# The transposed h of the last two packs, made from a transposed x by elementwise passes

## The chip, the cores and the metric

The kernel runs on one core of one Trainium2 chip. The metric is the device time of one execution in microseconds (us); the median of three runs of the kernel before is 2174.33 us (2174.08 to 2176.43). All data are 32-bit floats.

## What is computed

Two layers over a graph of 3327 nodes with 512 features. `_layernorm` has no weights of its own.

```
h = maximum(_layernorm(x), 0)
q, k, v = h @ Wq.T + bq, h @ Wk.T + bk, h @ Wv.T + bv
a = q @ k.T / sqrt(512) + adj + adj
x = x + softmax(a) @ v

h = maximum(_layernorm(x), 0)
A2 = adj + eye
dscale = diagonal(A2) ** -0.5
x = x + relu((dscale[:, None] * A2 * dscale[None, :]) @ (A2 @ h @ W.T))
```

The change concerns the first two lines: h, in the transposed form in which the query projection and the scores use it.

## The kernel before, in words

The nodes are padded to 26 tiles of 128 rows. A half holds 13 tiles. Matrix products are done in Strassen's manner (Winograd's form): of two halves of one side and two halves of the other, seven products of sums and differences in place of eight. The key projection is folded into the query side, M = Wq.T Wk, so that the scores are h (h M).T.

**First stage, to about 112 us.** The tiles of a half are put into four packs (`PACKS`, L213) of 4, 3, 3 and 3; a pack stands for its tiles in both halves, so 8, 6, 6 and 6 tiles. They are taken in the order `TURN` = (1, 2, 0, 3). "Third" and "fourth" below are pack 0 (8 tiles, products of 512 columns) and pack 3 (6 tiles, products of 384 columns).

`h_transposed(k)` (L304) makes a pack's transposed h in `hp[k]`, a tile of seven parts: a11, a12 (0, 1) from the first half of the nodes, a22 (2) from the second, and the sums S1 to S4 (3, 4, 5, 6), into which a21 goes. For each tile it loads x (L275, on SP's DMA queue, into a ring of 11 buffers), takes mean and variance on VectorE (`norm`, L191 to L200) with the power -1/2 on GpSimd (L200), applies scale, bias and Relu on ScalarE (L311) into `ht` (a ring of four buffers), stores `ht` to DRAM for the later stages (`rowd`, L312), turns it by four transposes on TensorE (`tp`, L315) into one bank of PSUM, and gets it out by copies on ScalarE (L318, L320) and sums on VectorE (L321, L322, and L324, L325 once for a pack).

`project_q(k)` (L327) multiplies a pack's seven parts by the seven parts of M, in two chains (o = 0, 1), one for each half of a quarter's outputs. The order within a chain is that of `Chain` (L231):

```
product(Y, "m1", True);  first(0, Y, -1)
product(Z, "p5", True);  first(3, Z, -1)
product(X, "p2", True);  more(0, X)
product(Y, "p6", False); first(1, Y, -1)
Chain.finish()
product(Z, "p3", False); more(1, Z)
product(Y, "p7", False); more(3, Y)
```

`Chain.finish()` does the p4, `first(2)` and `last()` of the chain before. X, Y and Z are banks of PSUM. A product with `False` adds to what its bank holds, so it must come after the read of the bank ahead of it. `first` is a read on ScalarE (L341), `more` a read on VectorE (L344); both write into `qs[0..3]` (L331), each of which has a single buffer, used again by the next pack. `last`, in the second chain alone, stores the four to DRAM (`qd`, L351) from SP's queue. As a chain's p4 and `last` come inside the next chain, those of a pack's second chain come inside the next pack.

The loop at L388 to L392 calls `h_transposed` for the next pack and then `project_q` for the one before it. In this stage the order of the instructions on each engine is chosen by a planner, which takes ready instructions by the order in which they were written; nothing is fixed by hand. So transposes of the next pack lie between the products of this one.

**Later stages.** The scores (from L397, products at L467) load the queries back from `qd` (`queries`, L404, into buffers `half` 0, 14, 1 and 2), and there and in the three large products after (L826, L818) every engine's order is fixed by hand with `in_order` (L91): each instruction is made to follow the one before it on its engine.

Of the kernel before, what the change touches and what calls it, by code (L numbers as in the profile page):

```python
# [35 lines left out]
HALF = 13  # L36
# [7 lines left out]
ROW = tuple(STRIPS[s] + y * HT[s] + k for y in range(2) for s in range(2) for k in range(HT[s]))  # L44
# [3 lines left out]
def graph_layers_kernel(  # L48
    ctx: ExitStack,
    tc: tile.TileContext,  # L50
    x: bass.AP,
    adjT: bass.AP,
    wq: bass.AP,
    wk: bass.AP,
# [22 lines left out]
    nc = tc.nc  # L77
# [28 lines left out]
    def half(k, shape, name):  # L106
        return arena.tile(shape, F32, name=name, tag=f"half{k}")
# [58 lines left out]
    totd = dram.tile([1, NP], F32, name="totd")  # L166
    x1d = [dram.tile([P, D], F32, name=f"x1d{i}") for i in range(NT)]
    rowd = [[dram.tile([P, D], F32, name=f"row{g}_{i}") for i in range(NT)] for g in range(3)]
    t2d = [[dram.tile([P, 4, P], F32, name=f"t2{g}_{t}") for t in range(PAIRS + 1)] for g in range(3)]

    def four_sums(o, g):
# [16 lines left out]
        lo, hi = max(r0, c0), min(r0 + P, c0 + a.shape[-1])  # L188
        return (slice(lo - c0, hi - c0), ident[:, lo - r0 : hi - r0]) if lo < hi else None

    def norm(src):  # L191

        st = small.tile([P, 6], F32, name="st")
        nc.vector.bn_stats(st, src)
        mv = small.tile([P, 2], F32, name="mv")
        nc.vector.bn_aggr(mv, st)
        ve = small.tile([P, 1], F32, name="ve")
        nc.vector.tensor_scalar(ve, mv[:, 1:2], EPS, None, op0=ALU.add)  # L198
        rstd = small.tile([P, 1], F32, name="rstd")
# [31 lines left out]
    class Chain:  # L231
# [72 lines left out]
    def h_transposed(k, tp_bank=tp_bank):  # L304

        a, n = PACKS[k]
        for _, i in (o for o in order if o[0] == k):
            xt = first.pop(i) if i in first else load_x(i)
            rstd, bias = norm(xt)
            ht = n_ring([P, D], "ht")  # L310
            nc.scalar.activation(ht, xt, AF.Relu, bias=bias(), scale=rstd)  # L311
            nc.sync.dma_start(rowd[0][ROW[i]], ht)  # L312
            pt = tp_bank("tp").rearrange("p (c e) -> p c e", c=DC)
            for c in range(DC):
                nc.tensor.transpose(pt[:, c], ht[:, c * P : (c + 1) * P], ident)  # L315
            w = slice((i % HALF - a) * P, (i % HALF - a + 1) * P)
            if i < HALF:
                nc.scalar.copy(hp[k][:, 0:2, :, w], pt.rearrange("p (a c) e -> p a c e", a=2))  # L318
            else:
                nc.scalar.copy(hp[k][:, 2, :, w], pt[:, 2:4])  # L320
                nc.vector.tensor_add(hp[k][:, 3, :, w], hp[k][:, 2, :, w], pt[:, 0:2])  # L321
                nc.vector.tensor_add(hp[k][:, 5, :, w], hp[k][:, 0, :, w], pt[:, 0:2])  # L322
            yield
        nc.vector.tensor_add(hp[k][:, 4], hp[k][:, 3], hp[k][:, 0])  # L324
        nc.vector.tensor_add(hp[k][:, 6], hp[k][:, 1], hp[k][:, 4])  # L325

    def project_q(k):  # L327
        a, n = PACKS[k]
        w = n * P

        qs = [half(8 + j, [P, 2, BW], "qs") for j in range(4)]  # L331

        def chain(o):
            def product(ps, name, start):
                for c in range(2):
                    nc.tensor.matmul(ps[:, :w], M[B[name]][:, c, o * P : (o + 1) * P], hp[k][:, A[name], c],  # L336
                                     start=start and c == 0, stop=c == 1, skip_group_check=True)

            def first(j, ps, sign):
                d = 2 * (j % 2) + o  # L340
                nc.scalar.activation(qs[j][:, o, :w], ps[:, :w], AF.Identity, bias=u[:, d : d + 1], scale=float(sign))  # L341

            def more(j, ps):
                nc.vector.tensor_add(qs[j][:, o, :w], qs[j][:, o, :w], ps[:, :w])  # L344

            def last():
                if o == 1:
                    for j in range(4):
                        y, z = divmod(j, 2)
                        i = ROW[y * HALF + a] * P  # L350
                        nc.sync.dma_start(qd[:, 2 * z : 2 * z + 2, i : i + w], qs[j][:, :, :w])  # L351

            Chain(product, first, more, last)

        for o in range(2):
            chain(o)
# [28 lines left out]
    for r in range(DC):  # L385
        nc.tensor.matmul(pu[:, r : r + 1], weighed[:, r * P : (r + 1) * P], ones, start=True, stop=True)
    nc.vector.tensor_scalar(u, pu[:, :DC], scale, None, op0=ALU.mult)
    for k, then in itertools.zip_longest(TURN, TURN[1:]):  # L388
        if then is not None:
            for _ in h_transposed(then):  # L390
                pass
        project_q(k)  # L392

# [358 lines left out]
    class Right:  # L752
# [78 lines left out]
    class Gather:  # L831
# [14 lines left out]
        def parts(self, of):  # L846

            return [of[k][:, w] for k, w in self.spots]
# [737 lines left out]
```

## Time and profile before

| | |
|---|---|
| median of three runs | 2174.33 us |
| the profiled execution | 2175.3 us |
| its span, first to last instruction | 2173.4 us |
| TensorE busy | 2158.9 us, 6400 matmul records |
| VectorE busy | 1667.4 us |
| ScalarE busy | 238.1 us |
| GpSimd busy | 47.3 us |
| transposes of the first stage (L315) | 104 records, one each |
| products of the first stage (L336) | first at 25.0 us, four records each: 1.29 us for 384 columns, 1.72 for 512 |
| first product of the scores (L467) | 112.4 us |

A matmul of 32-bit floats leaves two records, and a product has two matmuls. A line such as "PE Y L336 x4" names engine, tile written, line and count. "Idle before" and waits are put down to what came last. Busy time of one engine counts only its own instructions; the issue of a DMA is listed under its queue (SPq). Ends of matmuls are modelled, so neighbouring records can overlap.

### The profile page before, as it was taken

What the parts mean: (1) busy time and instruction counts of PE and PEld (TensorE: products, weight loads), DVE (VectorE), ACT (ScalarE), POOL (GpSimd) and SP (SyncE); (2) the same over time, 40 slices, a digit from 0 to 9 for tenths busy, and PEclk for the clock granted to TensorE, in tenths of its full rate; (3) what the DMA queues carried; (4) which work ended last, traced back from release to release, by engine and by line L of the source; (5) the groups of instructions that cost most, each with busy time, mean ns of one, the idle gap of its engine ahead of it and who ended that gap; (6) DMA issues with size and microseconds to landing.
All of it is one profiled execution on the core that took longest, in us unless ns stands there. A gap on an engine that the chain in (4) does not pass through costs nothing.

```text
span 2173.4 us, 21053 instructions
## 1 busy us (share of the span) xinstructions
PE 2158.9 (99%) x6400; PEld 1192.8 (55%) x6400; DVE 1667.4 (77%) x3254; ACT 238.1 (11%) x363; POOL 47.3 (2%) x60
## 2 busy tenths in 40 slices
PE   9999999999999999999999999999999999999998
PEld 5555555455555555555454555555666655555555
DVE  7379888888886698886778778887676667778686
ACT  5312121111110000000000000000011100000011
POOL 2000000000000000000111000000000000000000
PEclk9999999999999999999999999999999999999999
DMA  8478888888989899888787889986646468766685
GB/s 300 168 245 295 301 298 286 303 286 298 320 288 304 291 375 332 286 298 302 260 304 262 308 279 370 320 302 219 209 143 200 141 203 277 253 189 213 217 304 197
DMA packets 300374, 583.68 MB, mean 269 GB/s; under 512 B 34518, under 2 KB 168028, under 8 KB 300252
## 3 DMA queue, kind: packets, MB, share of 16 engines
q1 hardware_dynamic: 264958, 512.76, 69.9%
q10 hardware_dynamic: 35294, 69.48, 8.7%
q8 instruction: 53, 0.87, 0.2%
q14 instruction: 69, 0.57, 0.1%
HBM read 414.28 MB, written 167.85 MB: 268 GB/s over the span
## 4 chain that ended last, share of the span: by engine, by line
PE 93%; DVE 4%; DMA 2%; issue 1%; ACT 0%; POOL 0%; SPq 0%; ACTq 0%; DVEq 0%; POOLq 0%
PE p L826 54%; PE Y L467 13%; PE Z L467 6%; PE p L818 5%; PE p L918 4%; PE pw L979 3%; PE X L467 3%; PE Y L336 2%; PE Z L336 1%; DMA part<-sum 1%; DVE part L173 1%; PE pt L1008 1%; PE X L336 0%; DMA rows<-row 0%; PE tp L315 0%
## 5 line engine op out<-in xcount | busy, mean ns | idle before, releaser
L826 PE MATMUL p<-part,b 128*128 128x448 f32 (+1 forms) x3528 | 1261.6, 513 | 0.3 <-DVE part L871 0.2
L826 PEld LDWEIGHTS p<-part,b 128*128 128x128 f32 x3528 | 668.0, 190 | 534.9 <-issue 285.3
L467 PE MATMUL Y<-qt,hp 128*128 128x448 f32 (+1 forms) x832 | 308.3, 513 | 1.1 <-DVE g L479 1.0
L173 DVE TENSOR_TENSOR part<-part 128x896 f32<-128x896 f32 (+1 forms) x252 | 257.2, 1021 | 63.1 <-DMA part<-p 30.1
L467 PEld LDWEIGHTS Y<-qt,hp 128*128 128x128 f32 x832 | 157.7, 190 | 135.5 <-issue 72.3
L467 PE MATMUL Z<-qt,hp 128*128 128x384 f32 (+1 forms) x416 | 162.5, 513 | 0.0
L175 DVE TENSOR_TENSOR part<-part,part 128x448 f32<-128x448 f32 (+1 forms) x219 | 129.5, 591 | 15.3 <-DVE part L174 0.5
L174 DVE TENSOR_TENSOR part<-part,part 128x448 f32<-128x448 f32 (+1 forms) x219 | 129.4, 591 | 7.2
L818 PE MATMUL p<-part,b 128*128 128x448 f32 (+1 forms) x336 | 124.2, 513 | 0.0
L467 PEld LDWEIGHTS Z<-qt,hp 128*128 128x128 f32 x416 | 78.8, 190 | 67.4 <-issue 37.2
L471 DVE SCALAR_TENSOR_TENSOR g<-g,Y 128x384 f32<-128x384 f32 (+1 forms) x156 | 91.6, 587 | 31.2 <-PE Y L467 27.6
L818 PEld LDWEIGHTS p<-part,b 128*128 128x128 f32 x336 | 63.7, 190 | 53.5 <-issue 31.8
L854 ACT COPY part<-p 128x384 f32<-128x384 f32 (+1 forms) x33 | 16.6, 502 | 657.4 <-PE p L826 570.7
L474 ACT ACTIVATE g<-g 128x768 f32<-128x768 f32 (+1 forms) x48 | 43.0, 896 | 349.5 <-DVE g L471 286.0
L467 PE MATMUL X<-qt,hp 128*128 128x384 f32 (+1 forms) x208 | 81.1, 513 | 0.0
L918 PE MATMUL p<-w,ct 128*128 128x512 f32 x136 | 61.8, 594 | 0.5 <-DVE part L930 0.5
L855 DVE TENSOR_TENSOR part<-p,part 128x384 f32<-128x384 f32 (+1 forms) x33 | 19.3, 586 | 55.1 <-PE p L826 54.4
L467 PEld LDWEIGHTS X<-qt,hp 128*128 128x128 f32 x208 | 39.5, 190 | 33.1 <-issue 19.3
L979 PE MATMUL pw<-w,rows 128*128 128x256 f32 x208 | 53.6, 380 | 0.8 <-DVE rows L969 0.8
L200 POOL TENSOR_TENSOR rstd<-ve,mhalf 128x1 f32<-128x1 f32 x52 | 41.4, 797 | 566.3 <-DVE ve L198 529.4
L909 DVE TENSOR_TENSOR job<-job 128x896 f32<-128x896 f32 (+1 forms) x52 | 53.0, 1019 | 0.1
L479 DVE TENSOR_TENSOR g<-g,Z 128x384 f32<-128x384 f32 (+1 forms) x52 | 30.5, 586 | 26.6 <-PE Z L467 26.4
(178 smaller groups left out, 1692.8 us busy)
## 6 DMA issues: line engine op xcount, KB each, us to landing
part<-sum SPq DMA_DIRECT2D x104, 448.0 KB, 5.4
part<-p SPq DMA_DIRECT2D x91, 448.0 KB, 5.9
part<-sum SPq DMA_DIRECT2D x104, 384.0 KB, 3.6
part<-p SPq DMA_DIRECT2D x91, 384.0 KB, 4.4
part<-in_adjT_dram SPq DMA_DIRECT2D x78, 448.0 KB, 4.8
b<-row SPq DMA_DIRECT2D x234, 128.0 KB, 4.7
part<-in_adjT_dram SPq DMA_DIRECT2D x78, 384.0 KB, 3.8
g<-in_adjT_dram SPq DMA_DIRECT2D x52, 448.0 KB, 4.2
```

Source lines behind the costliest of these rows:

```text
L173: yield nc.vector.tensor_add(o[:, 0:2], g[:, 0:4:3], g[:, 1:2].to_broadcast([P, 2, g.shape[-1]]))
L174: yield nc.vector.tensor_add(o[:, 2], o[:, 1], g[:, 0])
L175: yield nc.vector.tensor_add(o[:, 3], o[:, 2], g[:, 2])
L336: nc.tensor.matmul(ps[:, :w], M[B[name]][:, c, o * P : (o + 1) * P], hp[k][:, A[name], c], start=start and c == 0, stop=c == 1, skip_group ...
L467: nc.tensor.matmul(ps[:, :wd], h_of(self.t, name, k), qt[B[name]][:, k], start=start and k == 0, stop=k == 1, skip_group_check=True)
L471: nc.vector.scalar_tensor_tensor(a[n], a[n], 2.0, ps[:, :wd], op0=ALU.mult, op1=ALU.add if sign > 0 else ALU.subtract)
L474: nc.scalar.activation(g[1], g[1], AF.Exp, **({"bias": pad} if self.t == HALF - 1 else {}))
L818: yield nc.tensor.matmul(ps[("p2", "p3", "p4", "p8")[k]][:, :w], b[:, z], a[:, 0, y], start=k == 3, stop=True)
L826: yield nc.tensor.matmul(ps[r][:, :w], b[:, i], m, start=self.t == 0, stop=self.t == PAIRS - 1 and r in ("p1", "p5", "p6", "p7"))
L909: nc.vector.tensor_add(self.a, self.a, self.b)
L918: nc.tensor.matmul(ps, cts[s][y][d][:, k * P : (k + 1) * P], w[d], start=d == 0, stop=d == DC - 1)
L979: nc.tensor.matmul(ps, a, W[B[name]][:, c], start=new and c == 0, stop=c == 1, skip_group_check=True)
```

## The change

The kernel gets a second input, `xT`, which is x (padded) transposed on the host. For the first two packs all is as before. For the third and fourth a class `Turned` takes the place of `h_transposed`:

- `__init__`: x, norm, Relu into `ht` and the store of `ht` for each tile as before, no transposes; the means and the powers -1/2 of the pack's tiles are kept side by side in `stats`.
- `turn`: two transposes on TensorE turn the means and the powers into rows, ScalarE copies them, and SP stores them to DRAM (`normd`).
- `load`: four loads of blocks of `xT` (into a11, a12, a buffer for a21, and a22), placed on SP's queue behind the pack's last store of `ht`, and two loads that spread the stored rows over all partitions.
- `parts`: two subtractions of the mean on GpSimd (a11, a12), and ten passes on VectorE: subtract and scale-with-Relu for a22, a21, scale for a11, a12, and the four sums.

`project_q` takes a list of such steps, `beside`, and does one behind each read of a bank (`place`) from the place numbered `late` on. A pack has 14 places: six in its first chain, then first(0), first(3), more(0), first(1), first(2) of the first chain, more(1), more(3), and one inside the next pack. The third's `turn` and `load` are done at place 9 (counted from 0) of pack 1; its passes at places 4 to 12 of pack 2, the last of them after; the fourth's `turn` and `load` follow between pack 2 and pack 0, and its passes lie in pack 0 in the same way. The stores of `qs` are placed on SP's queue behind the last of these loads that was written (`behind`). TensorE's order is fixed by hand from the projection of pack 1 on, VectorE's from that of pack 2 on.

```diff
-    def norm(src):
+    def norm(src, kept=None):
...
-        mv = small.tile([P, 2], F32, name="mv")
+        mv = small.tile([P, 2], F32, name="mv") if kept is None else kept
...
-        rstd = small.tile([P, 1], F32, name="rstd")
+        rstd = small.tile([P, 1], F32, name="rstd") if kept is None else kept[:, 1:2]
...
+        def turn(self):
+            k, stats, n = self.k, self.stats, PACKS[self.k][1]
+            pt, by_row = tp_bank("tp"), half(3, [P, P], "by_row")
+            for m in range(2):
+                nc.tensor.transpose(pt[: 2 * n, m * P : (m + 1) * P], stats[:, m], ident)
+                rows = by_row[32 * m : 32 * m + 2 * n]
+                nc.scalar.copy(rows, pt[: 2 * n, m * P : (m + 1) * P])
+                nc.sync.dma_start(normd[k][m][0, : 2 * self.w].rearrange("(i p) -> i p", p=P), rows)
+
+        def load(self):
+            k, w = self.k, self.w
+            self.other = half(2, [P, 2, BW], "a21")[:, :, :w]
+            a11, a12, a22 = hp[k][:, 0], hp[k][:, 1], hp[k][:, 2]
+            for y, blocks in enumerate(((a11, a12), (self.other, a22))):
+                c0 = ROW[y * HALF + PACKS[k][0]] * P
+                xs = xT[:, c0 : c0 + w].rearrange("(z c p) e -> z p c e", z=2, p=P)
+                for z, to in enumerate(blocks):
+                    after(nc.sync.dma_start(to, xs[z]), self.row)
+            self.norms = []
+            for m in range(2):
+                self.norms.append(half(m, [P, 2, BW], "norms")[:, :, :w])
+                self.loaded = nc.sync.dma_start(
+                    self.norms[m], normd[k][m][0:1, : 2 * w].rearrange("a (y e) -> a y e", y=2).to_broadcast([P, 2, w]))
+
+        def parts(self):
+            o, (a11, a12, a22, s1, s2, s3, s4) = self.other, (hp[self.k][:, j] for j in range(7))
+            mean, by = ([e[:, y : y + 1].to_broadcast([P, 2, self.w]) for y in range(2)] for e in self.norms)
+            nc.gpsimd.tensor_sub(a11, a11, mean[0])
+            nc.gpsimd.tensor_sub(a12, a12, mean[0])
+
+            def scaled(v, y):
+                return nc.vector.scalar_tensor_tensor(v, v, 0.0, by[y], op0=ALU.max, op1=ALU.mult)
+
+            yield nc.vector.tensor_sub(a22, a22, mean[1])
+            yield scaled(a22, 1)
+            yield nc.vector.tensor_sub(o, o, mean[1])
+            yield scaled(o, 1)
+            yield nc.vector.tensor_add(s1, a22, o)
+            yield scaled(a11, 0)
+            yield nc.vector.tensor_add(s2, s1, a11)
+            yield scaled(a12, 0)
+            yield nc.vector.tensor_add(s4, a12, s2)
+            yield nc.vector.tensor_add(s3, a11, o)
+
-    def project_q(k):
+    def project_q(k, beside=iter(()), late=0):
...
+        def place():
+            if next(places) >= late:
+                next(beside, None)
...
                         i = ROW[y * HALF + a] * P
-                        nc.sync.dma_start(qd[:, 2 * z : 2 * z + 2, i : i + w], qs[j][:, :, :w])
+                        ins = nc.sync.dma_start(qd[:, 2 * z : 2 * z + 2, i : i + w], qs[j][:, :, :w])
+                        if behind:
+                            after(ins, behind[-1])
...
-    for k, then in itertools.zip_longest(TURN, TURN[1:]):
-        if then is not None:
-            for _ in h_transposed(then):
-                pass
-        project_q(k)
+    for _ in h_transposed(TURN[1]):
+        pass
+    third = Turned(TURN[2])
+    behind = []
+
+    def norms_of_third():
+        third.turn()
+        third.load()
+        behind.append(third.loaded)
+        yield
+
+    with in_order(nc.tensor.engine):
+        project_q(TURN[0], norms_of_third(), 9)
+    fourth = Turned(TURN[3])
+    with in_order(nc.vector.engine, nc.tensor.engine):
+        parts = third.parts()
+        project_q(TURN[1], parts, 4)
+        for _ in parts:
+            pass
+        fourth.turn()
+        fourth.load()
+        behind.append(fourth.loaded)
+        parts = fourth.parts()
+        project_q(TURN[2], parts, 4)
+        for _ in parts:
+            pass
+        project_q(TURN[3])
```

More of the change, by code (lines that the diff above doesn't have):

```diff
@@ L51, in graph_layers_kernel @@
     x: bass.AP,
+    xT: bass.AP,
     adjT: bass.AP,
@@ L168, in graph_layers_kernel @@
     rowd = [[dram.tile([P, D], F32, name=f"row{g}_{i}") for i in range(NT)] for g in range(3)]
+    normd = {k: [dram.tile([1, 2 * 4 * P], F32, name=f"norm{m}_{k}") for m in range(2)] for k in range(4)}
     t2d = [[dram.tile([P, 4, P], F32, name=f"t2{g}_{t}") for t in range(PAIRS + 1)] for g in range(3)]
@@ L325, in h_transposed, with after, __init__ @@
         nc.vector.tensor_add(hp[k][:, 6], hp[k][:, 1], hp[k][:, 4])
-    def project_q(k):
+    def after(ins, other):
+        tc.add_manual_dep(ins.ins, other.ins.name,
+                          mybir.DependencyInfo(mybir.DependencyClass.NoSync, mybir.DependencyReason.DATA),
+                          reason="in_order")
+    class Turned:
+        def __init__(self, k):
+            self.k, (a, n) = k, PACKS[k]
+            self.w = n * P
+            stats = small.tile([P, 2, 8], F32, name="stats", bufs=2)[:, :, : 2 * n]
+            for _, i in (o for o in order if o[0] == k):
+                xt = load_x(i)
+                rstd, bias = norm(xt, stats[:, :, i // HALF * n + i % HALF - a])
+                ht = n_ring([P, D], "ht")
+                nc.scalar.activation(ht, xt, AF.Relu, bias=bias(), scale=rstd)
+                self.row = nc.sync.dma_start(rowd[0][ROW[i]], ht)
+            self.stats = stats
+        def turn(self):
[37 more added lines that the diff above has]
+            yield nc.vector.tensor_add(s3, a11, o)
@@ L331, in project_q @@
         qs = [half(8 + j, [P, 2, BW], "qs") for j in range(4)]
+        places = itertools.count()
+        def place():
+            if next(places) >= late:
+                next(beside, None)
         def chain(o):
@@ L341, in first @@
                 nc.scalar.activation(qs[j][:, o, :w], ps[:, :w], AF.Identity, bias=u[:, d : d + 1], scale=float(sign))
+                place()
             def more(j, ps):
                 nc.vector.tensor_add(qs[j][:, o, :w], qs[j][:, o, :w], ps[:, :w])
+                place()
             def last():
@@ L1562 @@
         "x": padded(x),
+        "xT": turned(padded(x)),
         "adj": plain(adj),
@@ L1580 @@
             bad = flag.tile([1, 1], mybir.dt.int32, name="bad")
-            x_in, adj_in, *rest = args
-            with tc.If(graph_layers_kernel(tc, x_in, *rest, out, bad) > 0):
+            x_in, xT_in, adj_in, *rest = args
+            with tc.If(graph_layers_kernel(tc, x_in, xT_in, *rest, out, bad) > 0):
                 general_kernel(tc, x_in[: x.shape[0]], adj_in, *rest, out)
```

## The prediction

> **What bounds the kernel now.** First the page: engines' busy shares, then who holds TensorE (PE) up (waiter, what it waited for, us in total, times, longest).
>
> ```profile
> PE 2158.9 (99%) x6400; PEld 1192.8 (55%) x6400; DVE 1667.4 (77%) x3254; ACT 238.1 (11%) x363; POOL 47.3 (2%) x60
> PE tp L315 <- ACT hp L318: 1.8, 1, 1.8
> PE Y L467 <- DVE g L479: 1.0, 1, 1.0
> ```
>
> PE is busy 2158.9 of 2173.4 us, and its longest waits are these two, the first at 22.74 us, ahead of the projection. A microsecond of PE work taken out before 112 us (where the scores' products, L467, begin) is therefore a microsecond of the end, if no new wait appears. Then ten-us windows (length, busy us of PE, PEld, DVE, ACT, POOL, clock, DMA share, GB/s):
>
> ```profile
> 20.00:30.00 10.00, 8.00 (x38) 5.30 (x37) 9.60 (x26) 8.70 (x21) 2.12 (x4) 0.83 0.97 325
> 30.00:40.00 10.00, 10.00 (x40) 6.18 (x40) 9.52 (x37) 7.47 (x14) 3.26 (x6) 1.00 0.86 281
> 40.00:50.00 10.00, 10.00 (x46) 6.62 (x45) 7.89 (x29) 4.85 (x11) 2.31 (x5) 1.00 0.69 252
> 60.00:70.00 10.00, 10.00 (x40) 6.22 (x39) 2.41 (x5) 4.07 (x8) 0.00 (x0) 1.00 0.41 134
> 80.00:90.00 10.00, 10.00 (x24) 4.37 (x23) 3.02 (x4) 2.90 (x4) 0.00 (x0) 1.00 0.38 127
> ```
>
> VectorE (DVE) and the DMA engines are nearly full to 40 us and half idle after 60. What the change removes is seen in the chain of work that ended last (start, us, what); every transpose is one record:
>
> ```profile
> 66.48 1.29 PE Y L336 x4
> 67.77 0.87 PE tp L315 x8
> 68.65 0.86 PE Y L336 x2
> ```
>
> Eight transposes take 0.87 us (0.109 each), and a product of a 384-column pack (four records) 1.29. Last, the tile qs between the projection and its store, and who waited for it:
>
> ```profile
>   DMA qd<-qs: 1.7, 1
> DMA to landing us min/median/max: 2.4/2.7/4.6
> ```
>
> So a store of qs lands 2.7 us after its issue, and ScalarE (ACT) already waited once for such a landing, without harm to PE: qs has a single buffer per quarter.
>
> [...] 2.7 us when idle, 5.3 for x tiles in the full first 40 us. [...] PE idle from 22.74 to 24.50 us, and Y's six records from 25.16 took 3.63 us where 1.94 is normal.
>
> **The change, part by part.** [...]
>
> *Removed.* 14 tiles x 4 = 56 transposes x 0.109 = 6.1 us of PE, and the 0.14 us PE gap at 51.3: 6.2. Also on ACT 7 x 0.595 + 7 x 0.379 = 6.8 us of copies, on DVE 14 x 0.415 + 1.22 + 1.23 + 2 x 0.95 = 10.2 us; neither limits.
>
> *Added to PE.* Four transposes of statistics, 0.44. The second of each pair writes the bank from which ACT copies the first; whether it waits isn't shown before. Low end 0; high end a copy and two hand-overs, 0.28 (from 0.379 for 256 columns, 0.595 for 512) + 0.4 = 0.7 a pair. I take 0.2 a pair: 0.8 in all. The third's statistics must be there: the 20th power (L200) ran at 41.05 to 41.6 us before, the turn comes at 41.9, and these tiles now stand ahead of pack 1's bank reads for the planner: nothing, at worst 0.7 if neighbours' columns of the shared statistics tile make VectorE wait for GpSimd (0.55 an operation). The fixed order at 25 us forbids PE the early m1 matmul with which it bridged that spot: 0 to 0.6, I take 0, as transposes of pack 2 can stand there.
>
> *Added to DVE and GpSimd (POOL).* Ten passes of 1024 columns at 1.22 (row of L324) and ten of 768 at 0.95: 21.7 us. From the first place (behind p3 of the pack's first half, L252) PE has eight products, 10.3 us, before the next pack's m1 wants the sixth pass; six passes and the bank reads between them take 6 x 1.2 + 2 x 0.5 = 8.2. In windows of which DVE filled 2.4 to 4.8 us of 10 this fits: nothing, unless inputs land over 2 us late. POOL's two subtractions a pack have no like in the trace[...]. They may also slow DVE at their side[...]: nothing, at worst 2.
>
> *DMA.* Third: four loads of xT at 0.52 MB and two broadcasts of 0.52 MB; fourth: the same at 0.39 MB. With the row stores kept, 5.5 MB more, 14 us at the 385 GB/s of full windows. The third pack's come while the engines are full to 44 us.
>
> *The queue of SP, which decides.* Each pack's stores of qs are now issued behind the broadcast loads of the pack after next (pack 1's behind the third's, pack 2's behind the fourth's), and these wait for the landing of the statistics' own store. The waiting issue holds all behind it on SP. Behind the stores wait ACT's first writes into the same qs (L341), and behind the first of them PE: p6 adds to the bank Y that this read must have emptied (L244, L249). PE's order is now written down, so it can do nothing else.
>
> *First wait.* The statistics of the third are turned behind p6 of pack 1's second half, at 41.9 us in the trace of before (call it t). Till pack 2's p6 PE then has p4, p3, p7, m1, p5, p2: 6 x 1.29 = 7.7, so it is wanted at t + 8.0. The store of the first qs stands in the rings behind 2.1 MB of xT and 1.05 MB of broadcasts: 3.15 + 0.39 = 3.54 MB, 9.2 us at 385 GB/s, from about t - 0.5 (behind the last row store), and 1.7 us from last byte to landing (2.7 less 1.0 of transfer): t + 10.4. ACT's read 0.58 and hand-overs 0.3: t + 11.3. Wait 3.3 us. Low end 1.1, if xT is through already: copies 0.9, store 2.4, two broadcasts 0.8 of issue and 2.7 of transfer, qs 1.0 + 0.4, ACT 0.9: t + 9.1. High end 6.8 (rival 2).
>
> *Second wait.* For the fourth the turn comes at the end of pack 2, T. Pack 0's m1, p5, p2 at 1.72 each and the 0.2 put p6 at T + 5.4. Copies and first issue T + 0.7; landing of both stores T + 3.3; broadcasts issued to T + 3.9, moved (0.79 MB, 2.0 us) by about T + 6; store of qs 1.0 us and landing T + 7.2; ACT 0.69 + 0.2: T + 8.1. Wait 2.7, ends 1.8 and 3.7 (one xT load waits for a buffer freed by the third's last pass and may stand ahead). In the kernel before, these stores needed no such chain.
>
> *Clock.* [...] one halved window of 3.4 us costs 1.7. I take one, ends 0 and two.
>
> *Moved at no cost:* loads of queries(0) use the buffers of the fourth's broadcasts, free near 92 us, landed near 97 (x: 5.3); they are needed at 112.
>
> Sum: -6.2 + 0.8 + 3.3 + 2.7 + 1.7 = +2.3 us. Profiled execution: 2175.3 (2173.4 span + 1.9 around) + 2.3 = 2177.6; it lies 1.0 above the median of the runs, 2174.33, so the prediction is 2176.6: the gain is eaten by waits.
>
> **Rivals.** (1) *The landings come in time*, by xT being issued well before the turn and stores landing in 2 us: only 6.2 - 0.6 is left, 2168.7. For it: DMA is half idle from 44 us in the old trace, and statistics could be ready by 38 us. Against it: three landings in series don't fit 5.4 us at T. (2) *Slower: traffic ahead of the first qs store.* The fourth's row stores (four buffers, 4 x 0.26 MB, 2.7 us) are ready from 40 us on and may be issued ahead, with the last x loads behind them (0.8 us): the first wait becomes 3.3 + 3.5 = 6.8, with a second halved window 1.7: 2176.6 + 5.2 = 2181.8. It decides as soon as 0.8 us more than the forecast's 3.54 MB stand ahead and the second window is halved (over 4.35 us lost). For it: DMA share 0.93 to 0.99 at 40 to 44 us before. Against it: SP may place these row stores later. (3) *DVE late:* xT lands over 2.4 us behind the first place, the pinned passes stop the bank reads queued behind them, and PE waits as long again, 3 us more than in (2): 2185. Against it: the same lateness holds PE, and so the place, up first.
>
> **How the numbers follow.** Forecast 0.47 (own range 2171 to 2178.6), rival 1 0.20, rival 2 0.28, rival 3 0.05. 0.2% is 4.35 us, about what a measurement of this kernel can tell from no change: faster 0.20, same 0.47, slower 0.33. The range reaches from rival 1 to behind rival 2, 2168.5 to 2183.5.
>
> **What would show it.** Right: no transposes L315 after 46 us; PE waits for ACT's qs read twice, about 3 us each, ahead of p6 of packs 2 and 0; ACT's qs waits for the DMA qd<-qs there; the clock at 0.5 for a window after; scores' first product near 114 in place of 112.4 us. Wrong: that product near 107 with no such waits (rival 1), or DVE idle before a subtraction (rival 3).

## The result and the profile after

The changed kernel takes 2192.7 us (median of 6 runs, 2190.4 to 2197.6), the kernel before 2175.1 us beside it (6 runs, 2174.1 to 2176.4): ratio 1.0082, 95% interval 1.0072 to 1.0092, some 17.6 us slower. The forecast was 2176.6, its range ended at 2183.5. The profiled execution of the changed kernel took 2197.57 us (span 2195.8), the slowest of its six, so the difference of the two spans, 22.4 us, overstates by some 5 us; I compare medians, and use the trace for places.

The page's first part (busy us, share, instructions) shows that the change did what it says: TensorE has 52 records less.

```profile
PE 2160.7 (98%) x6348; PEld 1190.9 (54%) x6348; DVE 1678.3 (76%) x3256; ACT 234.4 (11%) x353; POOL 56.9 (3%) x64
```

No transposes of h (L317 in this file) come after 36 us, as forecast. The busy sum of PE still rose by 1.8 us: work at a halved clock counts as longer work (eight records 5.16 us in place of 2.74, below). TensorE's waits (waiter, what for, us in total, times, longest):

```profile
PE Y L409 <- ACT qs L414: 16.6, 3, 11.2
PE Y L566 <- DVE g L578: 2.1, 1, 2.1
PE tp L354 <- ACT by_row L356: 1.5, 2, 1.1
PE Z L409 <- DVE hp L323: 0.8, 1, 0.8
```

The first line is the two forecast waits, at 11.2 and 4.84 us in place of 3.3 and 2.7, and one of 0.57. The windows between 50 and 100 us (same columns as in the prediction):

```profile
50.00:60.00 10.00, 3.80 (x12) 1.90 (x10) 0.89 (x2) 0.00 (x0) 4.22 (x2) 0.80 0.96 349
60.00:70.00 10.00, 5.00 (x9) 2.72 (x10) 3.13 (x13) 3.84 (x6) 2.03 (x4) 0.52 0.94 326
80.00:90.00 10.00, 7.30 (x20) 3.07 (x18) 6.24 (x8) 0.51 (x2) 2.58 (x2) 1.00 0.53 172
90.00:100.00 10.00, 7.43 (x13) 3.48 (x14) 0.85 (x2) 2.64 (x4) 0.98 (x1) 0.66 0.32 121
```

Before, TensorE was busy all of 60 to 70 us at full clock, with the DMA engines at 0.41 and 134 GB/s. Now ScalarE does nothing from 50 to 60 us, the clock is at 0.80 and 0.52, and the DMA engines are full (0.96, 0.94). TensorE's timeline there (start, length, engine, line, records, in brackets the wait ahead):

```profile
41.84 1.45 PE L409 MATMUL X<-hp,M 128*128 128x384 f32 x4
...
44.42 0.27 PE L354 MATMUL tp<-ident,stats 128*8 128x128 f32 x1
45.78 0.27 PE L354 MATMUL tp<-ident,stats 128*8 128x128 f32 x1 [1.10 <-ACT by_row L356]
...
52.34 1.45 PE L409 MATMUL X<-hp,M 128*128 128x384 f32 x4
65.00 5.16 PE L409 MATMUL Y<-hp,M 128*128 128x384 f32 x8 [11.20 <-ACT qs L414]
...
92.57 5.46 PE L409 MATMUL Y<-hp,M 128*128 128x512 f32 x8 [4.84 <-ACT qs L414]
...
131.80 1.45 PE L566 MATMUL Y<-qt,hp 128*128 128x384 f32 x4
```

In the trace of before, for comparison: X of pack 1's second chain, and the lengths of eight such records at full clock.

```profile
39.26 1.45 PE L336 MATMUL X<-hp,M 128*128 128x384 f32 x4
...
57.29 2.74 PE L336 MATMUL Y<-hp,M 128*128 128x384 f32 x8
...
75.41 3.17 PE L336 MATMUL Y<-hp,M 128*128 128x512 f32 x8
```

Both waits are ahead of p6, of pack 2 and of pack 0, as forecast. The eight records behind each take 5.16 and 5.46 us; eight such records take 2.74 and 3.17 at full clock. The first product of the scores comes at 131.8 us in place of 112.4. Its 19.4 us add up from the trace: transposes -6.2, four transposes of statistics +0.4, their bank waits +1.5, the two waits +11.2 and +4.8, half speed behind them +2.4 and +2.3 (5.16 and 5.46 less the old lengths), the start +2.6 (X of pack 1's second chain at 41.84, before at 39.26): 19.0. The rest of the span's 22.4 us lies far behind: 1.1 more at L566, and 3.4 us at a granted clock of 0.50 from 650 us on, which cost 1.7 and which the traces of e6 and e7 do not have.

What the first wait is made of is seen on ScalarE and on SP's queue (an issue's length includes its own waits):

```profile
62.07 2.40 ACT L346 ACTIVATE ht<-xt,nb,stats 128x512 f32<-128x512 f32 x3 [12.89 <-DVE ve L200]
64.39 0.56 ACT L414 ACTIVATE qs<-Y,u 128x384 f32<-128x384 f32 x1
...
91.83 0.69 ACT L414 ACTIVATE qs<-Y,u 128x512 f32<-128x512 f32 x1 [8.96 <-DMA qd<-qs]
```

```profile
48.22 0.91 SPq L371 DMA_DIRECT2D norms<-norm  x2
49.19 1.40 SPq L347 DMA_DIRECT2D row<-ht  x3
50.68 2.83 SPq L277 DMA_DIRECT2D xt<-in_x_dram  x3
55.77 2.34 SPq L426 DMA_DIRECT2D qd<-qs  x3
...
86.27 0.37 SPq L367 DMA_DIRECT2D a<-in_xT_dram  x1
86.69 1.68 SPq L426 DMA_DIRECT2D qd<-qs  x3
```

Pack 1's first store of qs is issued only at 55.77 us, behind the broadcasts, three stores of ht and three loads of x of the fourth pack. It landed at 61.9 us. At the second place it stands behind the load of a21, which waited for VectorE's last pass. And two things ended late at the first place: the store, and three Relus of the fourth pack, which stand ahead of the read of the bank on ScalarE and wait for the statistics of x tiles that landed 8.4 to 8.9 us after their issue. The Relus ended at 64.5 us, so they held the read 2.5 us longer than the landing did. Why the store was issued 2.2 us after the last x load is in SP's own waits:

```profile
SPq L426 <- DMA norms<-norm: 3.0, 2, 2.2
SPq L277 <- DMA hp<-in_xT_dram: 0.9, 1, 0.9
```

A store of qs has no business with the broadcast of the statistics. But the trace shows that issues here come at a fixed distance behind landings: each of the five issues at 51.84, 53.19, 55.77, 57.06 and 57.76 us came 0.06 us behind the landing of the eighth transfer before it on the queue (51.78, 53.13, 55.71, 57.00 and 57.70 us). For the store it is the first broadcast, landed at 55.71.

That wait held the issue; that it held the landing is not shown. These transfers landed in the order of their issue, one close behind another: the last xT block at 53.13 us, the broadcasts at 55.71 and 57.00, the three stores of ht at 57.70 to 58.94, the three x loads at 59.60 to 60.91 (some 0.65 us for each 0.26 MB), the store of qs at 61.91. In e1, below, the store was issued 2.0 us sooner after the turn and landed 0.5 us later after it. So the bytes ahead of the store, and not the time of its issue, account for its landing in these two traces; no run takes that wait of the issue away alone.

### The profile page after: what moved, and what is told of

It is laid out like the page before. It is cut to its first block, busy times and chain, and to the rows that moved or that the text cites. A ratio compares the mean times of both kernels' runs of the same rounds, so it can differ in the third digit from the quotient of the medians.

```text
span 2195.8 us, 20965 instructions
## 1 busy us (share of the span) xinstructions
PE 2160.7 (98%) x6348; PEld 1190.9 (54%) x6348; DVE 1678.3 (76%) x3256; ACT 234.4 (11%) x353; POOL 56.9 (3%) x64
## 4 chain that ended last, share of the span: by engine, by line
PE 92%; DVE 4%; DMA 1%; issue 1%; ACT 0%; SPq 0%; POOL 0%; DVEq 0%; ACTq 0%
PE p L925 54%; PE Y L566 13%; PE Z L566 7%; PE p L917 5%; PE p L1017 4%; PE pw L1078 3%; PE X L566 3%; PE Y L409 1%; DMA xt<-in_x_dram 1%; PE Z L409 1%; DVE st L196 1%; PE pt L1107 1%; DVE part L175 0%; PE tot L619 0%; DVE part L176 0%
## 5 line engine op out<-in xcount | busy, mean ns | idle before, releaser
L566 PE MATMUL Y<-qt,hp 128*128 128x448 f32 (+1 forms) x832 | 309.6, 515 | 2.1 <-DVE g L578 2.1
L566 PEld LDWEIGHTS Y<-qt,hp 128*128 128x128 f32 x832 | 158.2, 191 | 136.5 <-issue 72.9
L566 PE MATMUL Z<-qt,hp 128*128 128x384 f32 (+1 forms) x416 | 162.6, 513 | 0.0
L566 PEld LDWEIGHTS Z<-qt,hp 128*128 128x128 f32 x416 | 78.8, 190 | 67.4 <-issue 37.2
L566 PE MATMUL X<-qt,hp 128*128 128x384 f32 (+1 forms) x208 | 81.1, 512 | 0.0
L409 PE MATMUL Y<-hp,M 128*128 128x384 f32 (+1 forms) x128 | 53.3, 558 | 16.6 <-ACT qs L414 16.6
L566 PEld LDWEIGHTS X<-qt,hp 128*128 128x128 f32 x208 | 39.5, 190 | 33.1 <-issue 19.3
```

The source lines that it names most:

```text
L566: nc.tensor.matmul(ps[:, :wd], h_of(self.t, name, k), qt[B[name]][:, k], start=start and k == 0, stop=k == 1, skip_group_check=True)
```

## The experiments

Three theories were open. **A**: the store of qs, single buffer, lands late on a queue full of other transfers. **B**: ScalarE's queue, the Relus ahead of the read. **C**, the prediction's own: the new ordering of the stores behind the broadcasts (`behind`). Then came the question what else eats the gain. "Before" stands at 2175.1 to 2175.6 us (23 to 45 runs) beside these kernels.

### x of the fourth pack early (e1_x_early)

```diff
     third = Turned(TURN[2])
+    xts = {i: load_x(i) for k, i in order if k == TURN[3]}
...
-    fourth = Turned(TURN[3])
+    fourth = Turned(TURN[3], xts)
```

> The fourth pack's x tiles are loaded ahead of the xT loads; nothing else. Theory A (store): PE's first wait, 11.2 us at p6 of pack 2, is the landing of pack 1's store of qs; it comes no earlier, so the wait stays at 7 to 11 us and the time within 4 us of 2192.7. Theory B (ScalarE's queue): the wait is that of the fourth's last three Relus, which stand ahead of the read on ScalarE and wait for x tiles that landed at 59.6 us; with x early they are done before 52 us, the wait falls to what the store leaves of it, 3 to 7 us, and the time by 4 to 8 us. The second wait, 4.8 us at p6 of pack 0, stays under both.

Measured: 2194.2 us (2191.5 to 2198.6), ratio 1.0091 (1.0074 to 1.0108): no gain. ScalarE:

```profile
58.38 1.52 ACT L346 ACTIVATE ht<-xt,nb,stats 128x512 f32<-128x512 f32 x2 [7.95 <-DMA row<-ht]
61.21 0.58 ACT L414 ACTIVATE qs<-Y,u 128x384 f32<-128x384 f32 x1 [1.32 <-DMA qd<-qs]
```

The Relus are done by 60 us (the last two waited for the four buffers of ht), and the read then waits for the landing of the store, which took 8.7 us from its issue at 52.42. p6 comes at 61.85 in place of 65.00 us, after 9.05 us of waiting: the wait is nearly all the store's now. In this trace the scores begin 2.0 us earlier than in the changed kernel's (129.79 us). The medians do not show it: the profiled execution is the fastest of e1's four, that of the changed kernel the slowest of its six, and both scatter by 7 us.

### A second set of buffers for pack 2's qs (e2_qs_twice)

```diff
-        qs = [half(8 + j, [P, 2, BW], "qs") for j in range(4)]
+        if k == TURN[1]:
+            qs = [kind(j, [P, 2, w], "qs") for kind, j in ((mid, 4), (mid, 5), (half, 12), (half, 3))]
+        else:
+            qs = [half(8 + j, [P, 2, BW], "qs") for j in range(4)]
...
-            pt, by_row = tp_bank("tp"), half(3, [P, P], "by_row")
+            pt, by_row = tp_bank("tp"), const.tile([P, P], F32, name="by_row")
```

> Pack 2 writes its qs into four other buffers, so that no read waits for a store of the pack before. Theory A: both waits (11.2 and 4.8 us) go, and with them two or three halved clock windows of 1.7 us: 2171 to 2176. Theory B: the second wait goes, and the first only as far as fewer Relus stand ahead of the read (two in place of three, of tiles loaded earlier): 2176 to 2186.

Measured: 2178.0 us (2175.5 to 2182.1), ratio 1.0009 (1.0000 to 1.0018), 14.7 us less than the changed kernel. Both waits ahead of p6 are gone, yet the time lies above the 2171 to 2176 us that theory A allowed. TensorE, with the two p6 first:

```profile
52.00 2.74 PE L412 MATMUL Y<-hp,M 128*128 128x384 f32 x8
...
76.33 3.17 PE L412 MATMUL Y<-hp,M 128*128 128x512 f32 x8
```

What is left of waits:

```profile
27.37 0.93 PE L412 MATMUL Z<-hp,M 128*128 128x384 f32 x2 [2.56 <-DVE hp L323]
...
69.69 0.37 PE L354 MATMUL tp<-ident,stats 128*6 128x128 f32 x1 [3.01 <-ACT by_row L356]
...
102.75 1.56 PE L412 MATMUL Z<-hp,M 128*128 128x384 f32 x4 [0.93 <-ACT qs L417]
```

The x loads are where the change has them, and yet the read of p6's bank no longer stands behind the Relus: as it need not wait for a store, the planner puts it ahead of them. (`by_row` is moved in the edit because its buffer is given to qs.) The order on ScalarE, B, was itself a consequence of the late store. The wait of B reappears at the fourth's statistics, whose copy stands behind a late Relu: 3.0 us.

### Both (e3_x_and_qs)

The two edits together.

> Both edits together. Under either theory no wait is left at p6 of packs 2 and 0: the removed transposes show, less the slower start (about 2.6 us) and the waits at the statistics' transposes (1.5 us): 2170 to 2174. If the time stays above 2178 both theories miss something.

Measured: 2176.4 us (2174.0 to 2180.6), ratio 1.0006 (0.9997 to 1.0015), above the 2170 to 2174 us that were expected. The 3.0 us fell to 0.43. Left: 2.94 at the start, 0.79 at the third's statistics, and 1.33 ahead of m1 of pack 0, for a pass of VectorE, with a stretch at half clock from 70.4 us behind it (granted clock 0.83 over 70 to 80 us) that cost 1.8 us more.

### Without the ordering (e4_free_stores)

```diff
-                        if behind:
-                            after(ins, behind[-1])
```

> The stores of qs are no longer ordered behind the loads of the statistics. The order on SP's queue is the same as in the changed kernel down to pack 1's stores, and differs only at pack 2's. So the first wait stays (9 to 12 us) under both theories; the second falls from 4.8 us to under 2 us if pack 2's stores stood in a chain of landings, with a halved window less: 2186 to 2190. If the prediction's reading of the first wait (the ordering puts pack 1's stores behind) were right, the first would fall below 5 us as well: below 2183.

Measured: 2187.8 us (2185.5 to 2191.4), ratio 1.0061 (1.0044 to 1.0077), 4.9 us less.

```profile
63.20 5.49 PE L409 MATMUL Y<-hp,M 128*128 128x384 f32 x8 [11.32 <-ACT qs L414]
...
86.29 3.17 PE L409 MATMUL Y<-hp,M 128*128 128x512 f32 x8
```

```profile
53.99 2.55 SPq L426 DMA_DIRECT2D qd<-qs  x3
```

The second wait is gone, the first is as long as ever: the planner issues pack 1's stores behind the same transfers without being told to. Theory C holds for pack 2's stores alone. The 2.0 us by which p6 of pack 2 comes earlier than in the changed kernel were won at the start (X of pack 1's second chain at 39.87 us), ahead of all stores that this edit frees.

### Pack 1's stores on GpSimd's queue (e9_pool)

```diff
-                        ins = nc.sync.dma_start(qd[:, 2 * z : 2 * z + 2, i : i + w], qs[j][:, :, :w])
+                        ins = (nc.gpsimd if k == TURN[0] else nc.sync).dma_start(qd[:, 2 * z : 2 * z + 2, i : i + w], qs[j][:, :, :w])
```

> The changed kernel, but pack 1's four stores of qs are issued from GpSimd's queue in place of SP's. Theory A (these stores come late because they stand on SP's queue behind the loads of xT, the two broadcasts and three loads of x, and each issue there waits for the landing of the transfer eight before it): the store of the first qs lands near 50 to 54 us in place of 61 to 65, the first wait of TensorE falls from 11.2 to 0 to 3 us, and the total falls by 8 to 13 us, to 2180 to 2185. Rival B (ScalarE's queue, with three Relus of the fourth pack ahead of the read, sets the first wait): those Relus end near 62 to 64 us as before, the wait stays near 11 us and the total at 2191 to 2193.

Measured: 2186.5 us (2186.0 to 2189.2), ratio 1.0052 (1.0034 to 1.0070), 6.2 us less. GpSimd's queue, ScalarE and TensorE:

```profile
47.16 0.90 POOL L426 DMA_DIRECT2D qd<-qs  x1
```

```profile
54.83 0.58 ACT L414 ACTIVATE qs<-Y,u 128x384 f32<-128x384 f32 x1 [6.06 <-DMA qd<-qs]
```

```profile
55.47 4.54 PE L409 MATMUL Y<-hp,M 128*128 128x384 f32 x8 [2.36 <-ACT qs L414]
...
85.32 5.45 PE L409 MATMUL Y<-hp,M 128*128 128x512 f32 x8 [6.53 <-ACT qs L414]
```

Issued 8.6 us earlier, the store ends the first wait after 2.4 us in place of 11.2. Its landing still takes 7.7 us, beside 2.1 MB of xT and 1.05 MB of broadcasts. The read also stands ahead of the Relus here, which come from 63.5 us on. So the place in SP's queue, with what it did to ScalarE's order, made 8.8 us of the wait; the landing among full DMA engines made the rest. Less than expected of it was left at the end, since the second wait grew to 6.5. Theory A stands: queue first, traffic second.

### The fourth's a21 in a buffer of its own (e7_own_a21)

```diff
-            self.other = half(2, [P, 2, BW], "a21")[:, :, :w]
+            self.other = half(2 if k == TURN[2] else 12, [P, 2, BW], "a21")[:, :, :w]
```

> The changed kernel, but a21 of the fourth pack gets a buffer of its own (half 12) in place of the one that the third pack's last pass frees. Theory A (the second wait, 4.84 us ahead of p6 of pack 0, is longer than forecast because this load waits on SP's queue for VectorE's last pass at 86.2 us and the stores of qs stand behind it): the second wait falls to about 2 to 3.5 us; the first stays near 11 us; total down by 1 to 3 us, 2189 to 2191.5. Rival (the stores come late by the landing of the statistics alone): the second wait stays at 4.5 to 5 us and the total at 2192 to 2193.

Measured: 2192.5 us (2190.2 to 2194.7), ratio 1.0076 (1.0060 to 1.0091): no change beyond the scatter. Two of its lines:

```profile
64.94 5.49 PE L409 MATMUL Y<-hp,M 128*128 128x384 f32 x8 [12.34 <-ACT qs L414]
...
91.98 6.34 PE L409 MATMUL Y<-hp,M 128*128 128x512 f32 x8 [3.69 <-ACT qs L414]
```

The second wait fell by 1.15 us, to 3.69, which is the load's share; the records behind it took 0.88 us more at half speed, so little was left. The first line tells something else: here the start happened to be 1.3 us earlier (X of pack 1's second chain at 40.55), the first wait is 1.14 us longer, and p6 of pack 2 comes at 64.94 us, where the changed kernel has 65.00.

### No fixed order round pack 1's projection (e6_start)

```diff
-    with in_order(nc.tensor.engine):
-        project_q(TURN[0], norms_of_third(), 9)
+    project_q(TURN[0], norms_of_third(), 9)
```

> The changed kernel, but without the fixed order of TensorE round the projection of pack 1: the planner may again slip one matmul of that pack ahead of others at the start. Theory A (the fixed order cost about 3 us at the start, because Z then waits for the sum on VectorE and a second clock window is halved): the X product of pack 1's second chain begins 2 to 3 us earlier (near 39 us, where the changed kernel has 41.8), and the total falls by about as much, 2189 to 2191, unless the first wait takes it back, as that one ends with a store and not with TensorE; then the total stays at 2192 with a first wait 2 to 3 us longer. Rival (the start is late by the traffic of transposes or by chance of the clock): nothing changes at the start.

Measured: 2193.3 us (2192.0 to 2194.1), ratio 1.0082 (1.0064 to 1.0100). X of pack 1's second chain begins at 39.22 us, 2.6 earlier, as theory A said, and the wait takes more than half of it back:

```profile
63.92 5.31 PE L409 MATMUL Y<-hp,M 128*128 128x384 f32 x8 [13.61 <-ACT qs L414]
```

So little of what is won at the start arrives behind a wait that ends with a store: 1.1 of 2.6 us here, none of 1.3 in e7, though 1.8 of 2.0 in e4. Nor are the 2.6 us the price of the fixed order alone. With it the same X begins at 41.84 us in the changed kernel, at 39.87 to 41.17 in e1, e2, e3, e4, e7 and e9; between 25 and 33 us the changed kernel's trace has 6.8 us at half clock, e6, e9 and the kernel before have 3.4, e7 none; by the lengths of their records e4 lost 1.6 us there (four records 2.50 us in place of 1.46, two 1.37 in place of 0.81) and e1 none. No run separates the order from the clock.

### Four edits, and where VectorE's passes lie (e8_all, e11_late3, e10_noX)

e8_all: early x, second buffers for qs, no fixed order at the start, and

```diff
             for m in range(2):
+                if m:
+                    pt = tp_bank("tp")
                 nc.tensor.transpose(pt[: 2 * n, m * P : (m + 1) * P], stats[:, m], ident)
```

> Four edits to the changed kernel: x of the fourth pack loaded ahead of pack 1's projection, a second set of buffers for pack 2's qs, a bank of its own for the second statistics transpose, and no fixed order of TensorE round pack 1's projection. With the first two alone the median was 2176.4, with waits of 2.9 at the start, 1.3 ahead of m1 of pack 0 and 1.2 at the statistics left. Theory A (every lost microsecond stands in these waits and in the halved clock behind them): start and statistics go, 2171 to 2173, faster than the kernel before by 2 to 4 us. Rival (the waits only move, to the next thing that is late, VectorE's passes): 2175 to 2177.

Measured: 2174.6 us (2172.5 to 2179.5), ratio 0.9998 (0.9990 to 1.0007), above the 2171 to 2173 that were expected. The waits at the statistics' banks are gone. 2.0 us are left ahead of m1 of pack 0, for a pass of VectorE. Its timeline, and then GpSimd's:

```profile
55.24 1.22 DVE L385 TENSOR_TENSOR hp<-hp,norms 128x1024 f32<-128x1024 f32 x1
...
56.85 2.92 DVE L383 SCALAR_TENSOR_TENSOR hp<-hp,norms 128x1024 f32<-128x1024 f32 x1
59.69 3.37 DVE L387 TENSOR_TENSOR a<-a,norms 128x1024 f32<-128x1024 f32 x1
63.09 1.22 DVE L383 SCALAR_TENSOR_TENSOR a<-a,norms 128x1024 f32<-128x1024 f32 x1
```

```profile
55.28 3.41 POOL L379 TENSOR_TENSOR hp<-hp,norms 128x1024 f32<-128x1024 f32 x1 [4.64 <-DMA norms<-norm]
58.64 3.34 POOL L380 TENSOR_TENSOR hp<-hp,norms 128x1024 f32<-128x1024 f32 x1
```

Passes that take 1.22 us alone took 2.92 and 3.37 while GpSimd subtracted, and GpSimd's 2.33 became 3.4. In the changed kernel the two never met, because the passes came 17 us later, behind the first wait.

e11_late3 begins the passes one place earlier (3 in place of 4):

> The same four edits, and the passes of VectorE begin one place earlier (place 3 in place of 4) in packs 2 and 0. Theory A (the wait of 1.3 us ahead of m1 of pack 0 is for a pass that has its inputs, and is just placed late): that wait goes and the total is 1 to 2 us below that of the four edits alone. Rival (the pass waits for the landing of xT and of the broadcasts): the wait stays, or bank reads behind the waiting pass are held, and the total is the same or 1 to 3 us higher.

Measured: 2177.1 us (2174.2 to 2180.9), ratio 1.0006 (0.9999 to 1.0013). The wait ahead of m1 is 2.6 us, not shorter, though VectorE's passes were begun one place earlier: the place was not the matter.

e10_noX leaves x where the change has it:

> Three of the four edits: a second set of buffers for pack 2's qs, a bank of its own for the second statistics transpose, no fixed order of TensorE round pack 1's projection; x of the fourth pack is loaded where the change has it. Theory A (loading x early crowds the DMA engines and VectorE at 20 to 30 us and costs a clock window there): the start is 1 to 2 us earlier than with all four, the passes beside GpSimd's subtractions still hold m1 of pack 0 by about 2 us; 2173 to 2175. Rival (without the early x the statistics of the fourth come late, its Relus stand ahead of reads on ScalarE): a wait of 2 to 3 us at the turn of the fourth, 2176 to 2178.

Measured: 2175.4 us (2170.6 to 2179.3), ratio 0.9999 (0.9992 to 1.0006). The waits at the fourth's statistics come back (0.6 and 2.1, for VectorE and GpSimd), as the rival said, with 1.1 ahead of m1. X of pack 1's second chain begins at 38.49 us, 1.6 earlier than in e8, as theory A said; but it is at 38.48 in e11 too, with the early x. What differs is the clock: between 25 and 35 us it was at half for 3.4 us in e8 (granted 0.82 and 0.84 in two windows of five us), and at 1.00 throughout in these two. So theory A was right on the start and wrong on its cause.

### The subtractions on VectorE (e12_vsubs, e13_xvsubs)

```diff
-            nc.gpsimd.tensor_sub(a11, a11, mean[0])
-            nc.gpsimd.tensor_sub(a12, a12, mean[0])
...
+            yield nc.vector.tensor_sub(a11, a11, mean[0])
+            yield scaled(a11, 0)
             yield nc.vector.tensor_sub(a22, a22, mean[1])
...
-            yield scaled(a11, 0)
             yield nc.vector.tensor_add(s2, s1, a11)
+            yield nc.vector.tensor_sub(a12, a12, mean[0])
             yield scaled(a12, 0)
```

> As the run before it, and GpSimd's two subtractions of a pack become passes of VectorE, that of a11 with its scaling first. Theory A (in the version with all four edits two passes of VectorE took 2.92 and 3.37 us in place of 1.22 while GpSimd subtracted, 3.4 us in place of 2.33, and m1 of pack 0 waited 2.0 us for it): no pass is longer than 1.3 us, m1 doesn't wait, and the total is 1.5 to 3.5 us below that of the run before it, near 2171.5. Rival (VectorE has 2.4 us more to do in each pack, and its order is fixed): bank reads come late, waits of 1 to 2 us at p6 or p5 of pack 0, the total the same within 1 us.

Measured: 2174.5 us (2171.9 to 2178.2), ratio 0.9996 (0.9987 to 1.0004). Nothing waits ahead of m1, but p2 of pack 0 waits 2.5 us for the scaled a12, now the tenth of twelve passes, and a stretch at half clock follows (granted 0.83 over 70 to 80 us): the wait moved, as the rival said.

> All four edits, and the subtractions on VectorE as in the run before it. Theory A: 2 us below the four edits alone (2174.6), 2172 to 2173.5, with the loss at the start still there. Rival: no gain, 2174 to 2176.

Measured, with the early x too: 2171.0 us (2168.1 to 2175.8, 17 runs), ratio 0.9979 (0.9972 to 0.9987), 4.4 us below the kernel before and 1.0 below what was expected at best. The waits of TensorE that are left at the start and behind it, and two passes of VectorE:

```profile
28.11 1.68 PE L317 MATMUL tp<-ident,ht 128*128 128x128 f32 x8 [2.45 <-DVE hp L324]
...
69.82 1.98 PE L413 MATMUL X<-hp,M 128*128 128x512 f32 x4 [0.76 <-DVE hp L380]
```

```profile
57.57 1.22 DVE L380 SCALAR_TENSOR_TENSOR hp<-hp,norms 128x1024 f32<-128x1024 f32 x1
58.70 1.22 DVE L384 TENSOR_TENSOR hp<-hp,norms 128x1024 f32<-128x1024 f32 x1
```

No pass is longer than 1.23 us though VectorE does two more a pack, and the scores begin at 108.9 us in place of 112.4. Of the 6.2 us of removed transposes 3.5 arrive at the scores; 0.8 are lost at p2, 0.4 in the statistics' transposes and 1.3 at the start (X of pack 1's second chain at 40.51 against 39.26): 2.5, which leaves 3.7 by this sum. In e12 the start was 2.2 us earlier (38.35), but the scaled a12 of p2 was no earlier: it is done at 69.8 us in both. The passes of e12 do begin sooner (53.50 us against 55.96), yet statistics of the fourth pack, whose x comes late there, lie between them.

## Why the prediction was wrong

The mechanism was right in the main: stores of qs come late on SP's queue, the next write of qs on ScalarE waits for them, and p6 waits for that, twice. The size of the first wait was far off, and the reason given for it, the ordering that the change adds, was not the one at work there. The change came out slower by 17.6 us where some 2 were forecast.

- **Removed and added on TensorE** (-6.2, +0.8): right. Transposes are gone, a statistics transpose is 0.11 us. The waits for the bank were 1.10 and 0.44 us, against 0.2 a pair taken and 0.7 at most: 1.5 in place of 0.4. The first is above the high end; what it cost behind the first wait is not shown.
- **First wait** (+3.3, ends 1.1 and 6.8): the step that failed; measured 11.2. From the turn at t = 44.42 p6 was wanted at t + 9.4 (forecast 8.0) and came at t + 20.6 (forecast 11.3). Two terms of the sum were wrong. The first is "The store of the first qs stands in the rings behind 2.1 MB of xT and 1.05 MB of broadcasts", landing at t + 10.4. It landed at t + 17.5, 6.1 us after an issue at t + 11.4. Three stores of ht and three x loads (1.6 MB) stood ahead of it too, as rival 2 had it, and 326 to 349 GB/s were moved, not 385 (before, full stretches had 381 at 50 to 51 us and 387 at 74 to 76): with these two in it, the prediction's own sum gives t + 15.8 to t + 16.9 (an estimate). Moreover, three of the four xT loads were issued only at t + 2.3 to t + 3.3, behind the statistics' stores, where the sum began at t - 0.5. No run separates these parts. The second term is "ACT's read 0.58 and hand-overs 0.3": three Relus stood ahead of that read on ScalarE, and held it 2.5 us beyond the landing (64.5 against 61.9). The prediction looked at what SP's queue puts ahead of the store, and not at what ScalarE's puts ahead of the read.
- **"The queue of SP, which decides"**: SP's queue decides, but not by the ordering of the stores that the change adds. Without that ordering the first wait is 11.3 us (e4). With the stores on another queue it is 2.4 (e9), with other buffers it is gone (e2).
- **Second wait** (+2.7, ends 1.8 and 3.7): right in kind, measured 4.84. It is due to the ordering (gone in e4). The load of a21, put into the high end, is worth 1.15 (e7); the landing took 5.0 us where 2.7, the median of these stores before, had been taken.
- **Clock** (+1.7, ends 0 and two windows): two places, 2.4 and 2.3 us, each more than the 1.7 that was charged once. In the trace of before the granted clock was at 0.50 for 3.4 us (0.62, 0.50, 0.50 and 0.67 in the microseconds from 25 to 29), and six records took 3.63 us in place of 1.94: that is the 1.7. In the changed kernel the clock stood at 0.50 from 56.0 to 69.7 us, that is from 2.2 us into the first wait on, and from 90.2 to 97.0 us, from 2.5 us into the second. So 4.7 us of work from 65.00 us on and 4.4 from 92.57 us on ran at half speed, and about half of that is lost; I had charged a single stretch of 3.4. That a wait of 3.3 us would cost one such stretch was the author's estimate; what decides when the clock falls and when it comes back, the runs do not show.
- **"Fixed order at 25 us ... I take 0"**: the start was 2.6 us later than before, of which the order and the half clock there are not separated (e6); most of it vanishes in the first wait in the changed kernel, not so in its mended versions.
- **"The third's statistics ... nothing, at worst 0.7"**: for the third right; it was the fourth's, which the sum did not ask about, that cost 3.0 us as soon as the waits were away (e2).
- **Passes of VectorE and GpSimd "nothing, at worst 2"**: nothing in the changed kernel, 2.0 where the passes come in time (e8). GpSimd's subtractions took 2.34 us for 1024 columns and 1.80 for 768; the prediction had no measured figure for them, and its "at worst 2" was the author's estimate.
- **Rivals.** Rival 2 (traffic ahead of the first store) is what happened, decided as its text said by the stores of ht and the x loads; its price, 2181.8, lacked the later issue of the xT loads, the Relus, and the slower landings. Rival 3 (VectorE late) played no part.

As a sum: taking both waits and the clock behind them away (e2) gives 14.7 us back, where the forecast had 3.3 + 2.7 + 1.7 = 7.7. The other 8.3 us (from -5.4, what the forecast leaves without the waits, to e2's +2.9) are in e2's trace 3.0 at the fourth's statistics, 0.8 at the third's, 1.3 at the start (X at 40.51), 0.9 ahead of p3 and 1.3 at half clock behind the 3.0: 7.3 us, of which the forecast had 0.4 as waits for the banks. They are read from the trace; no run of its own separates them. Nor is it shown why the scores' L566 waits 1.1 us more in the changed kernel than before; in e8, e10 and e13 it waits 0.2 to 0.8.

## What to carry to other kernels

When a step is to overlap more, follow each single buffer from the last reader to the next writer through both queues: what stands ahead of the store on its queue, and what stands ahead of the next write on the engine's own. A second set of buffers for one tile (14.7 us here, against 4.9 in e4 and 6.2 in e9) was worth more than any reordering tried. A wait that ends with a transfer can swallow gains and losses ahead of it (1.1 of 2.6 us arrived in e6, none of 1.3 in e7): mend the last one in the chain first, then look again, since the next (bank, statistics, passes beside another engine's) only then shows.

## What the runs showed of the hardware that was not expected

- **VectorE and GpSimd stood in each other's way.** Passes of 1024 columns took 2.92 and 3.37 us in place of 1.22 beside GpSimd's subtractions, these 3.41 and 3.34 in place of 2.33 (e8; 2.34 in the changed kernel, where no such pass ran beside them). In order of time: the first subtraction starts 0.04 us behind a pass of 1.22 and takes 1.08 longer than its 2.33; the next pass starts at 56.85, 1.84 us before that subtraction ends, and takes 1.70 longer; the second subtraction takes 1.01 longer, and the pass behind it, started at 59.69, ends at 63.06, 1.1 us after that subtraction. With the subtractions on VectorE no pass took over 1.23 us (e13). By what the two engines hold each other up is not shown.
- **Landing took longer where more was in flight.** The stores of qs landed in 2.4 to 4.6 us before. In the changed kernel those issued at 55.8 to 57.8 us took 5.8 to 6.1 and those at 86.7 to 87.7 us 5.0 to 6.0, but the ones at 70.80 and 98.67 us 2.8 and 2.4. Where they were issued amid xT and the broadcasts (e9) they took 7.6 to 8.4. At 50 to 62 us of the changed kernel's trace the landings of SP's queue follow one another in the order of issue, 0.60 to 0.66 us for each 0.26 MB, so that the bytes ahead give the time there.
- **A wait can be dearer than its length.** Behind 11.2 and 4.84 us of waiting TensorE lost 2.4 and 2.3 us more at half clock. Behind 2.0 us (e8, 67.20 us) it lost none, and behind 0.43 and 1.33 us (e3) it lost 1.8: the length alone does not decide it.
